# Channel 0's filters shifted by TensorE, read from eight partitions, with products of zeros and other loads at the start

## The chip, the cores and the metric

One core of one Trainium2 chip. The metric is the device time of one execution in microseconds (us), lower is better; for the kernel before, the median of three runs is 884.42 us (883.73 to 887.07).

## The reference, cut to what is computed

Two layers in a row on x of shape (4, 64, 256, 256): 4 images (b), 64 channels (c), 256 by 256 places. All is fp32.

```
# layer 0: a long convolution whose filter is separable, one for each channel
h_X, h_Y = filter(z, X weights), filter(z, Y weights)      # 256 places x 64 channels each
filter: h = sin(freq * (z @ w1 + b1)); h = sin(freq * (h @ w2 + b2)); h = sin(freq * (h @ w3 + b3))
        (h @ wo) * exp(-t * |deltas|)
k[c, i, m] = h_X[i, c] * h_Y[m, c]
y = causal 2D convolution of x[b, c] with k[c], cut to 256 x 256 (the reference does it by FFTs of 512 x 512)
x0 = y + x * bias[c]

# layer 1
scores = x0 @ x0.T / 16                                    # for each image and channel, 256 x 256
red = sum over t of scores[s, t] * weights[c, s, t]        # one number for each row s
y = x0 + red
out = batch norm of y over (b, s, d) for each channel, times gamma[c], plus beta[c]
```

Because the filter is an outer product, the convolution is two products with triangular Toeplitz matrices, one along each axis: z = (Toeplitz of h_Y) on x, then x0 = (Toeplitz of h_X) on z.

## The kernel before

**Preparation (lines 84 to 173).** The small filter network runs once, for all channels, on a transposed z (33 x 256) in two halves of 128 places. For each of three layers and each half, TensorE (PE) multiplies by a 128 x 128 matrix that holds the X and Y weights as blocks (line 131), VectorE (DVE) adds the bias and scales (134), finds the nearest whole number of turns (138) and subtracts it (139), and ScalarE (ACT) takes the sine (141). The biases and the frequencies arrive in fb_sb; line 123 makes a factor of them first. What all 64 channels need then goes this way: a last product (158), times the decay (161), into g_sb; lines 170 write it to g_dram, a DRAM tensor with four copies, each copy's row read later from another start.

**Toeplitz tiles.** A channel's tile `toep` (tag of `hs[c]`) has 128 partitions, two filters (index a: 1 is used by conv_z, 0 by conv_x0) and 256 places: partition p holds the filter put p places on, and partitions 64 to 127 repeat 0 to 63. For channels from 1 on it is read from g_dram by four DMAs of 16 partitions (load_h, line 187), and ACT copies the lower half down (copy_h, line 192). Channel 0 doesn't wait for DRAM: lines 143 to 155 compute its two filters with the weights of that one channel on all 128 columns, so that each partition holds the same filter; two DMAs a filter then read one partition each (0 and 64) at 32 starts, one element apart, into partitions 0 to 31 and 32 to 63 of `hs[0]`. DVE copies these down (line 163). At the end of the preparation three products that nobody reads run on PE (lines 165 to 167, tile `idle`, one buffer).

**Channels.** For each channel, conv_z (line 210) multiplies blocks of xt, the input, by the Toeplitz tile; ACT copies the result from PSUM to the tile z (copy_z, line 219), in two halves m of two blocks each. conv_x0 (line 233) multiplies z by the Toeplitz tile; DVE adds x times the bias (line 240) and makes x0. `gram` (line 270) makes the scores, of which DVE takes the weighted sums (290, 294, 304), GpSimd the sums over partitions, and then means, squares, scaling and output follow for earlier channels. All products use quarters of the PE array: 64 rows and 64 columns, four beside each other.

**Order.** The order is written out by hand; nothing is planned. The loop of channel c issues conv_x0 of c, then conv_z of c + 1, then gram of c, so that PE always has work whose inputs are old. Before the loop stand conv_z of channel 0 and its copies. Loads are all issued on SyncE's queue (SP), in the order of the program: input tiles (load_xt) three channels ahead, Toeplitz rows two ahead, weights (load_w) one ahead. In the preparation ACT's queue carries the weights of the network, one of the two reads per filter of channel 0 and one of the two writes to g_dram. Each DMA takes one of eight semaphores, and an issue waits until the DMA that had it last is done.

**PSUM.** The preparation's pool `fps` uses four buffers for `ph`, three for `ph0` and one for the idle products; it is given back before `ps`, eight buffers of one bank, is opened for the channels. A conv_z or a conv_x0 takes four of them.

Of the kernel before, what the change touches and what calls it, by code (L numbers as in the profile page):

```python
# [16 lines left out]
P = 128  # L17
EMB = 33
# [19 lines left out]
def conv_scores_bn_kernel(  # L38
# [3 lines left out]
    wl: bass.AP,  # L42
    zT: bass.AP,
    fw: bass.AP,
# [38 lines left out]
    ctx.enter_context(tc.manual_schedule())  # L83
    zT_sb = const.tile([EMB, S], F32, name="zT_sb")
    nc.sync.dma_start(zT_sb, zT)
    fw_sb = const.tile([P, 4, P], F32, name="fw_sb")
    nc.scalar.dma_start(fw_sb[:EMB, 0, :], fw[:EMB, 0, :])
    fb_sb = const.tile([P, 4], F32, name="fb_sb")
    nc.sync.dma_start(fb_sb, fb)
    nc.scalar.dma_start(fw_sb[:, 1:, :], fw[:, 1:, :])  # L90
    eps = const.tile([P, 1], F32, name="eps")
    nc.vector.memset(eps, BN_EPS)
    ones = const.tile([P, H], F32, name="ones")
    nc.vector.memset(ones, 1.0)

    warm = const.tile([P, 1], F32, name="warm")
# [24 lines left out]
    hs[0] = ld.tile([P, 2, GW], F32, tag="toep", name="toep_0")  # L121
    with tc.tile_pool(name="fps", bufs=4, space=PSUM) as fps:
        nc.vector.tensor_scalar(turns, fb_sb[:, 3:4], 1.0 / (2.0 * math.pi), None, ALU.mult)

        halves = [zT_sb[:, bass.ts(n, P)] for n in range(2)]
        for layer in range(3):
            for n in range(2):
                rhs = halves[n]
                K = rhs.shape[0]
                ph = fps.tile([P, P], F32, tag="ph", name=f"ph_{layer}_{n}")  # L130
                nc.tensor.matmul(ph, lhsT=fw_sb[:K, layer, :], rhs=rhs, start=True, stop=True)  # L131

                a = wk.tile([P, P], F32, tag="fa", name=f"fa_{layer}_{n}")
                nc.vector.tensor_scalar(  # L134
                    a, ph, fb_sb[:, layer : layer + 1], turns, ALU.add, ALU.mult
                )
                k = wk.tile([P, P], F32, tag="fk", name=f"fk_{layer}_{n}")
                nc.vector.tensor_scalar(k, a, ROUND, None, ALU.add)
                nc.vector.scalar_tensor_tensor(a, k, ROUND, a, ALU.subtract, ALU.subtract)  # L139
                h = wk.tile([P, P], F32, tag="fh", name=f"fh_{layer}_{n}", bufs=4)  # L140
                nc.scalar.activation(h, a, AF.Sin, scale=-PI2)
                halves[n] = h
        for a in (1, 0):
            ph = fps.tile([P, S], F32, tag="ph0", name=f"ph0_{a}", bufs=3)
            for n in range(2):
                weights = fw_sb[:, 3, a * C : a * C + 1].to_broadcast([P, P])
                nc.tensor.matmul(  # L147
                    ph[:, bass.ts(n, P)], lhsT=weights, rhs=halves[n], start=True, stop=True
                )
            nc.vector.tensor_tensor(g0_sb[:, a, :S], ph, decay0_sb[:, a], ALU.mult)  # L150
            for n in range(2):
                row = g0_sb[H * n : H * n + 1, a, 32 * n :]
                src = bass.AP(row.tensor, row.offset, [row.ap[0], [1, 32], [1, S]])
                queue = nc.scalar if n else nc.sync
                queue.dma_start(hs[0][bass.ts(n, 32), a, :S], src)
        ph = fps.tile([P, S], F32, tag="ph0", name="ph_out", bufs=3)
        for n in range(2):
            nc.tensor.matmul(
                ph[:, bass.ts(n, P)], lhsT=fw_sb[:, 3, :], rhs=halves[n], start=True, stop=True
            )  # L160
        nc.vector.tensor_tensor(g_sb[:, :S], ph, decay_sb, ALU.mult)
        for a in (1, 0):
            nc.vector.tensor_copy(hs[0][H:, a, :S], hs[0][:H, a, :S])

        for n in range(3):
            idle = fps.tile([P, 3, P], F32, tag="idle", name=f"idle_{n}", bufs=1)
            nc.tensor.matmul(idle, lhsT=fw_sb[:, 3, :], rhs=fw_sb[:, 1:, :], start=True, stop=True)  # L167
    for a in (1, 0):
# [494 lines left out]
```

## Time and profile before

| What | Value |
|---|---|
| median of three runs | 884.42 us |
| profiled execution, its own time | 883.99 us |
| its span, first to last instruction | 882.2 us |
| mean granted clock of TensorE | 0.992 |
| DMA over the span | 169.68 MB, mean 192 GB/s |
| 0 to 16.8 us: PE busy | 11.23 us |
| 26.1 to 30.5 us: PE busy | 4.40 of 4.40 us |
| 200 to 300 us: PE busy | 99.84 of 100 us |
| 840 to 882 us: PE busy | 27.99 us |

The span is what the profiler saw of one execution, from its first to its last instruction; the time of the same execution is 1.8 us longer, which lies outside the instructions. The rows of stretches add up what PE did in them. A product in fp32 appears as two instructions, since PE passes over the data twice. On a timeline row stand start, length, engine, line, operation, tiles and count; in brackets, how long the engine had been idle and what ended it. SPq and ACTq are the queues on which DMAs are issued: a row's length there is the issue, not the transfer. Two tiles in the preparation are named g_sb and two decay_sb in the trace, since g0_sb and decay0_sb lose their number.

### The profile page before, as it was taken

To read this page: it belongs to the slowest core of one execution; us is meant where nothing else is said; L and a number is where in the kernel's file an instruction comes from. 1 tells how busy PE (TensorE), PEld (TensorE's weight loads), DVE (VectorE), ACT (ScalarE), POOL (GpSimd) and SP (SyncE) were. 2 spreads that over 40 slices of the span, in tenths; PEclk is the share of its full clock that TensorE was granted. 3 is DMA by queue.
4 is the path that set the end of the run, shared out by engine and by line. 5 is a ranking of instruction groups with operands and counts; after the bars stand their busy time and mean duration, and the time that the engine had idled before them with its cause. 6 is when DMAs were issued, how large, how long until landed. Compare 5 with 4: busy or idle time off the path is not lost.

```text
span 882.2 us, 55900 instructions
## 1 busy us (share of the span) xinstructions
PE 860.4 (98%) x24678; PEld 827.0 (94%) x24678; DVE 754.9 (86%) x2642; ACT 616.7 (70%) x1212; POOL 425.1 (48%) x195
## 2 busy tenths in 40 slices
PE   7999999999999999999999999999999999999993
PEld 5999999999999999999999999999999999999992
DVE  3588988998898898898898898898898898898885
ACT  2257767767777777776776776776776776776784
POOL 0236446546545545645645644645645545645600
PEclk9999999999999999999999999999999999999996
DMA  6525556556556556556556565556556556556534
GB/s 187 178 88 176 198 197 211 198 190 212 198 196 212 192 199 208 197 194 211 192 199 209 197 197 202 196 193 207 191 192 210 183 201 206 201 193 206 182 124 169
DMA packets 89913, 169.68 MB, mean 192 GB/s; under 512 B 10566, under 2 KB 11784, under 8 KB 89672
## 3 DMA queue, kind: packets, MB, share of 16 engines
q1 hardware_dynamic: 89116, 165.51, 55.5%
q8 instruction: 194, 3.18, 1.5%
q10 hardware_dynamic: 556, 0.61, 0.2%
q14 instruction: 47, 0.39, 0.1%
HBM read 98.18 MB, written 67.76 MB: 188 GB/s over the span
## 4 chain that ended last, share of the span: by engine, by line
PE 97%; DVE 1%; ACT 0%; issue 0%; DMA 0%; ACTq 0%; SPq 0%; DVEq 0%
PE p L210 32%; PE p L233 32%; PE g L270 32%; PE rp L341 0%; PE rp L346 0%; PE idle L167 0%; DVE x L355 0%; DMA fb_sb<-in_fb 0%; ACT o L406 0%; PE ph L147 0%; PE ph L131 0%; DVE fa L134 0%; DVE fa L139 0%; DVE junk L290 0%; ACT z L219 0%
## 5 line engine op out<-in xcount | busy, mean ns | idle before, releaser
L312 POOL PARTITION_ALL_REDUCE rd<-sp x61 | 373.5, 6122 | 183.8 <-DVE sp L304 183.8
L233 PE MATMUL p<-toep,z 64*64 64x256 f32 (+3 forms) x8192 | 300.6, 296 | 1.2 <-issue 1.0
L210 PE MATMUL p<-toep,xt 64*64 64x256 f32 (+3 forms) x8192 | 299.8, 296 | 0.4 <-issue 0.2
L233 PEld LDWEIGHTS p<-toep,z 64*64 64x64 f32 x8192 | 285.5, 133 | 14.4 <-issue 2.8
L270 PE MATMUL g<-x 64*64 64x192 f32 (+1 forms) x8192 | 298.1, 296 | 0.4 <-issue 0.3
L210 PEld LDWEIGHTS p<-toep,xt 64*64 64x64 f32 x8192 | 282.9, 133 | 12.2 <-PE idle L167 0.7
L270 PEld LDWEIGHTS g<-x 64*64 64x64 f32 x8192 | 283.3, 133 | 2.8 <-issue 1.0
L290 DVE SCALAR_TENSOR_TENSOR junk<-g,w 128x192 f32<-128x192 f32 x512 | 161.1, 352 | 86.5 <-PE g L270 86.5
L406 ACT ACTIVATE o<-x,sh,g 128x512 f32<-128x512 f32 x253 | 203.5, 808 | 0.0
L240 DVE SCALAR_TENSOR_TENSOR x<-xt,chan_sb,p 128x512 f32<-128x512 f32 x256 | 174.1, 742 | 9.0 <-PE p L233 9.0
L219 ACT COPY z<-p 128x512 f32<-128x512 f32 x256 | 134.7, 577 | 31.1 <-PE p L210 31.1
L366 ACT ACTIVATE sq<-x,mom 128x1024 f32<-128x1024 f32 x128 | 146.3, 1143 | 5.4 <-DVE x L355 2.0
L326 DVE SCALAR_TENSOR_TENSOR x<-x,rd 128x1024 f32<-128x1024 f32 x122 | 144.2, 1220 | 0.1
L304 DVE SCALAR_TENSOR_TENSOR sp<-eye_sb,red,pr 128x128 f32<-128x128 f32 x488 | 138.1, 346 | 0.0
L330 POOL PARTITION_ALL_REDUCE mom<-mom x61 | 24.3, 399 | 235.0 <-DVE x L326 230.9
L294 DVE SCALAR_TENSOR_TENSOR pr<-g,w 128x256 f32<-128x256 f32 x256 | 107.5, 420 | 0.0
L319 ACT COPY rd<-rd 64x512 f32<-64x512 f32 x61 | 37.6, 616 | 91.1 <-POOL rd L312 91.1
L361 ACT ACTIVATE mom<-mom 128x1 f32<-128x1 f32 x62 | 18.3, 295 | 77.3 <-POOL mom L330 77.3
L192 ACT COPY toep<-toep 64x512 f32<-64x512 f32 x63 | 38.9, 617 | 39.9 <-DMA toep<-g_dram 26.4
L290 DVE DVE_READ_ACCUMULATOR junk<-g,w 128x1 f32 x512 | 42.6, 83 | 0.0
L372 POOL PARTITION_ALL_REDUCE tot<-mom x62 | 29.7, 480 | 9.5 <-ACT sq L366 9.5
L366 ACT ACTIVATION_READ_ACCUMULATOR sq<-x,mom 128x1 f32 x128 | 23.8, 186 | 0.0
(60 smaller groups left out, 212.0 us busy)
## 6 DMA issues: line engine op xcount, KB each, us to landing
xt<-in_xT SPq DMA_DIRECT2D x256, 256.0 KB
out<-o SPq DMA_DIRECT2D x256, 256.0 KB
w<-in_wl SPq DMA_DIRECT2D x64, 320.0 KB
toep<-g_dram SPq DMA_DIRECT2D x252, 36.0 KB
g_dram<-g_sb SPq DMA_DIRECT2D x1, 320.0 KB
g_dram<-g_sb ACTq DMA_DIRECT2D x1, 320.0 KB
decay_sb<-in_decay SPq DMA_DIRECT2D x1, 256.0 KB
fw_sb<-in_fw ACTq DMA_DIRECT2D x1, 192.0 KB
```

The source lines that it names most:

```text
L210: nc.tensor.matmul(p1[u][bass.ts(v, H), k, : S - H * i], lhsT=xts[c, v][rows, i, bass.ts(2 * m + k, H)], rhs=toep[rows, 1, H * i : S], sta ...
L219: nc.scalar.copy(zs[c][:, u, bass.ts(m, 2), :], p1[u][:, :, ::-1])
L233: nc.tensor.matmul(p2[v][bass.ts(u, H), i, : S - H * k], lhsT=z[rows, u, k, bass.ts(2 * m + i, H)], rhs=toep[rows, 0, H * k : S], start=(k ...
L240: nc.vector.scalar_tensor_tensor(x0[:, v, part], xt[v][:, part], chan_sb[:, 0, c : c + 1], p2[v][:, :, ::-1], ALU.mult, ALU.add,)
L270: nc.tensor.matmul(gs[u][bass.ts(h, H), o, :], lhsT=xb[rows, v, i, m, :], rhs=xb[rows, v, i, t, :], start=(i == 0), stop=(i == 3),)
L290: nc.vector.scalar_tensor_tensor(junk, g[:, part, :], 1.0 / math.sqrt(S), w[:, 3 * n : 3 * n + 3, :], ALU.mult, ALU.mult, accum_out=red0[: ...
L294: nc.vector.scalar_tensor_tensor(pr[:, b].rearrange("p (t s) -> p t s", s=H), g[:, COL, :], 1.0 / math.sqrt(S), w[:, 6:10, :], ALU.mult, A ...
L304: nc.vector.scalar_tensor_tensor(sp[:, b, part], eye_sb, red0[:, b, n : n + 1], pr[:, b, part], ALU.mult, ALU.add,)
L312: nc.gpsimd.partition_all_reduce(rd.rearrange("p b s -> p (b s)"), sp.rearrange("p b s -> p (b s)"), P, RED.add)
L326: nc.vector.scalar_tensor_tensor(x0[:, v], x0[:, v], 1.0, rd[:, 2 * v, None, :].to_broadcast([P, 4, S]), ALU.mult, ALU.add, accum_out=mom[ ...
L366: nc.scalar.activation(sq, st8[c][0][:, v], AF.Square, bias=mom[:, 5:6], accum_out=mom[:, 6 + v : 7 + v])
L406: nc.scalar.activation(o, y, AF.Identity, bias=sh, scale=g)
```

## The change

- The transposed z and the first layer's weights are one input `zw` and one load on SP; fb_sb is loaded first on ACT's queue, then the other weights `fw`, now of three layers.
- A function `idle` makes products of `ones` (64 columns) by `zeros` that nobody reads: three of 256 columns ahead of the network, one of 64 columns after each of its six products, and seven of 256 columns at the end in place of three with `fw`.
- Channel 0's filters: the 128 output partitions of `ph0` are four groups of 32, and the products of group k are put 16 k places on, so that partition 32 k holds the filter 16 k places on; the rest of `ph0` is set to zero ahead of the network, and `decay0` is put on the same way. Each filter's two DMAs then read four partitions each (0, 32, 64, 96 and 1, 33, 65, 97) at 16 starts and write 64 partitions each, so both halves of `hs[0]` are written and DVE's copies go.
- Channel 0's `w` and channel 1's input are loaded after the writes to g_dram instead of ahead of the network.
- conv_x0 of channel 0 is `first_x0`: all four PSUM banks are taken at once, the products with the first half of z (k of 0 and 1) come first for all rows, then those with the second half, and DVE's additions come after each m of the second half.

The diff, with declarations and the host's arrays cut:

```diff
     ctx.enter_context(tc.manual_schedule())
-    zT_sb = const.tile([EMB, S], F32, name="zT_sb")
-    nc.sync.dma_start(zT_sb, zT)
-    fw_sb = const.tile([P, 4, P], F32, name="fw_sb")
-    nc.scalar.dma_start(fw_sb[:EMB, 0, :], fw[:EMB, 0, :])
+    zw_sb = const.tile([P, P + S], F32, name="zw_sb")
+    nc.sync.dma_start(zw_sb[:EMB], zw[:EMB])
     fb_sb = const.tile([P, 4], F32, name="fb_sb")
-    nc.sync.dma_start(fb_sb, fb)
-    nc.scalar.dma_start(fw_sb[:, 1:, :], fw[:, 1:, :])
+    nc.scalar.dma_start(fb_sb, fb)
+    fw_sb = const.tile([P, 3, P], F32, name="fw_sb")
+    nc.scalar.dma_start(fw_sb, fw)
     eps = const.tile([P, 1], F32, name="eps")
     nc.vector.memset(eps, BN_EPS)
     ones = const.tile([P, H], F32, name="ones")
     nc.vector.memset(ones, 1.0)
+    zeros = const.tile([P, S], F32, name="zeros")
+    nc.vector.memset(zeros, 0.0)
 
     warm = const.tile([P, 1], F32, name="warm")
     nc.scalar.activation(warm, eps, AF.Sin)
...
     nc.sync.dma_start(eye_sb, eye)
     chan_sb = const.tile([P, 3, C], F32, name="chan_sb")
     nc.sync.dma_start(chan_sb.rearrange("p a c -> p (a c)"), chan.to_broadcast([P, 3 * C]))
-    load_w(0)
-    for part in PARTS:
-        load_xt(1, *part)
     g_sb = const.tile([P, GW], F32, name="g_sb")
     nc.vector.memset(g_sb[:, S:], 0.0)
 
...
 
     hs[0] = ld.tile([P, 2, GW], F32, tag="toep", name="toep_0")
     with tc.tile_pool(name="fps", bufs=4, space=PSUM) as fps:
+        def idle(cols, number=1):
+
+            for _ in range(number):
+                none = fps.tile([H, S], F32, tag="none", name="none", bufs=1)
+                nc.tensor.matmul(
+                    none[:, :cols], lhsT=ones, rhs=zeros[:, :cols], start=True, stop=True
+                )
+
+        idle(S, 3)
+
+        SHIFT = 16
+        ph0s = [fps.tile([P, S], F32, tag="ph0", name=f"ph0_{a}", bufs=3) for a in range(2)]
+        for a in (1, 0):
+            nc.vector.memset(ph0s[a][:, S - 3 * SHIFT :], 0.0)
         nc.vector.tensor_scalar(turns, fb_sb[:, 3:4], 1.0 / (2.0 * math.pi), None, ALU.mult)
 
-        halves = [zT_sb[:, bass.ts(n, P)] for n in range(2)]
+        halves = [zw_sb[:EMB, bass.ts(1 + n, P)] for n in range(2)]
         for layer in range(3):
             for n in range(2):
                 rhs = halves[n]
-                K = rhs.shape[0]
+                weights = fw_sb[:, layer - 1, :] if layer else zw_sb[:EMB, :P]
                 ph = fps.tile([P, P], F32, tag="ph", name=f"ph_{layer}_{n}")
-                nc.tensor.matmul(ph, lhsT=fw_sb[:K, layer, :], rhs=rhs, start=True, stop=True)
+                nc.tensor.matmul(ph, lhsT=weights, rhs=rhs, start=True, stop=True)
+                idle(H)
 
                 a = wk.tile([P, P], F32, tag="fa", name=f"fa_{layer}_{n}")
                 nc.vector.tensor_scalar(
...
                 nc.scalar.activation(h, a, AF.Sin, scale=-PI2)
                 halves[n] = h
         for a in (1, 0):
-            ph = fps.tile([P, S], F32, tag="ph0", name=f"ph0_{a}", bufs=3)
+            ph = ph0s[a]
+            weights = fw_sb[:, 2, a * C : a * C + 1].to_broadcast([P, 32])
             for n in range(2):
-                weights = fw_sb[:, 3, a * C : a * C + 1].to_broadcast([P, P])
-                nc.tensor.matmul(
-                    ph[:, bass.ts(n, P)], lhsT=weights, rhs=halves[n], start=True, stop=True
-                )
+                for k in range(4):
+                    first = max(0, P * n - SHIFT * k)
+                    nc.tensor.matmul(
+                        ph[bass.ts(k, 32), first : P * (n + 1) - SHIFT * k], lhsT=weights,
+                        rhs=halves[n][:, first + SHIFT * k - P * n :], start=True, stop=True,
+                    )
             nc.vector.tensor_tensor(g0_sb[:, a, :S], ph, decay0_sb[:, a], ALU.mult)
+
             for n in range(2):
-                row = g0_sb[H * n : H * n + 1, a, 32 * n :]
-                src = bass.AP(row.tensor, row.offset, [row.ap[0], [1, 32], [1, S]])
+                rows = g0_sb[n : n + 97 : 32, a, :]
+                src = bass.AP(rows.tensor, rows.offset, [rows.ap[0], [1, SHIFT], [1, S]])
                 queue = nc.scalar if n else nc.sync
-                queue.dma_start(hs[0][bass.ts(n, 32), a, :S], src)
+                queue.dma_start(hs[0][bass.ts(n, H), a, :S], src)
         ph = fps.tile([P, S], F32, tag="ph0", name="ph_out", bufs=3)
         for n in range(2):
             nc.tensor.matmul(
-                ph[:, bass.ts(n, P)], lhsT=fw_sb[:, 3, :], rhs=halves[n], start=True, stop=True
+                ph[:, bass.ts(n, P)], lhsT=fw_sb[:, 2, :], rhs=halves[n], start=True, stop=True
             )
         nc.vector.tensor_tensor(g_sb[:, :S], ph, decay_sb, ALU.mult)
-        for a in (1, 0):
-            nc.vector.tensor_copy(hs[0][H:, a, :S], hs[0][:H, a, :S])
-
-        for n in range(3):
-            idle = fps.tile([P, 3, P], F32, tag="idle", name=f"idle_{n}", bufs=1)
-            nc.tensor.matmul(idle, lhsT=fw_sb[:, 3, :], rhs=fw_sb[:, 1:, :], start=True, stop=True)
+        idle(S, 7)
     for a in (1, 0):
         queue = nc.scalar if a else nc.sync
         queue.dma_start(
             g_dram[:, :, a, :].rearrange("n c g -> c n g"),
             g_sb[bass.ts(a, C), None, :].to_broadcast([C, COPIES, GW]),
         )
+    load_w(0)
+    for part in PARTS:
+        load_xt(1, *part)
     gam = const.tile([P, C], F32, name="gam")
     nc.vector.tensor_scalar(gam, chan_sb[:, 1, :], -0.5, None, ALU.mult)
 
...
     def conv_x0(c, z, parts=range(2)):
 
 
-        xt = [xts[c, v] for v in range(2)]
-        toep, x0 = hs[c], st8[c][0]
+        toep = hs[c]
+        if not c:
+            first_x0(z)
+            return
         for m in parts:
             p2 = [ps.tile([P, 2, S], F32, tag="ps", name=f"p2_{c}_{m}_{v}") for v in range(2)]
             for i in range(2):
...
                             lhsT=z[rows, u, k, bass.ts(2 * m + i, H)],
                             rhs=toep[rows, 0, H * k : S], start=(k == 0), stop=(k == 3),
                         )
-            for v in range(2):
-                part = bass.ts(m, 2)
-                nc.vector.scalar_tensor_tensor(
-                    x0[:, v, part], xt[v][:, part], chan_sb[:, 0, c : c + 1],
-                    p2[v][:, :, ::-1], ALU.mult, ALU.add,
-                )
+            add_bias(c, m, p2)
+
+    def add_bias(c, m, p2):
+        for v in range(2):
+            part = bass.ts(m, 2)
+            nc.vector.scalar_tensor_tensor(
+                st8[c][0][:, v, part], xts[c, v][:, part], chan_sb[:, 0, c : c + 1],
+                p2[v][:, :, ::-1], ALU.mult, ALU.add,
+            )
+
+    def first_x0(z):
+
+        toep = hs[0]
+        p2 = [
+            [ps.tile([P, 2, S], F32, tag="ps", name=f"p2_0_{m}_{v}") for v in range(2)]
+            for m in range(2)
+        ]
+        for half in range(2):
+            for m in range(2):
+                for i in range(2):
+                    for k in range(2 * half, 2 * half + 2):
+                        for t in range(4):
+                            v, u = t % 2, t // 2
+                            rows = bass.ts(v, H)
+                            nc.tensor.matmul(
+                                p2[m][v][bass.ts(u, H), i, : S - H * k],
+                                lhsT=z[rows, u, k, bass.ts(2 * m + i, H)],
+                                rhs=toep[rows, 0, H * k : S],
+                                start=(i == 0 and k == 0), stop=(i == 1 and k == 3),
+                            )
+                if half:
+                    add_bias(0, m, p2[m])
...
+    zw = np.zeros((P, P + S), np.float32)
+    zw[:EMB, P:] = a["L0_conv_z"][0, ::-1].T
+    decay0 = np.zeros((4, 32, 2, S), np.float32)
+    for k in range(4):
+        decay0[k, :, :, : S - 16 * k] = decay[::C, ::-1][:, 16 * k :]
+    decay0 = decay0.reshape(P, 2, S)
+    fw = np.zeros((P, 3, P), np.float32)
```

More of the change, by code (lines that the diff above doesn't have):

```diff
@@ L42, in conv_scores_bn_kernel @@
     wl: bass.AP,
-    zT: bass.AP,
+    zw: bass.AP,
     fw: bass.AP,
@@ L608 @@
     decay = np.concatenate([dec, dec / np.float32(FFT)], 0)
-    fw = np.zeros((P, 4, P), np.float32)
+    zw = np.zeros((P, P + S), np.float32)
[5 more added lines that the diff above has]
+    fw = np.zeros((P, 3, P), np.float32)
     fb = np.zeros((P, 4), np.float32)
@@ L613 @@
         lo, hi = i * C, (i + 1) * C
-        fw[:EMB, 0, lo:hi] = a[f"L0_conv_{n}w1"]
-        fw[lo:hi, 1, lo:hi] = a[f"L0_conv_{n}w2"]
-        fw[lo:hi, 2, lo:hi] = a[f"L0_conv_{n}w3"]
-        fw[lo:hi, 3, lo:hi] = a[f"L0_conv_{n}wo"]
+        zw[:EMB, lo:hi] = a[f"L0_conv_{n}w1"]
+        fw[lo:hi, 0, lo:hi] = a[f"L0_conv_{n}w2"]
+        fw[lo:hi, 1, lo:hi] = a[f"L0_conv_{n}w3"]
+        fw[lo:hi, 2, lo:hi] = a[f"L0_conv_{n}wo"]
         for j, b in enumerate(("b1", "b2", "b3")):
@@ L639 @@
         "wl": wl,
-        "zT": a["L0_conv_z"][0, ::-1].T,
+        "zw": zw,
         "fw": fw,
@@ L643 @@
         "decay": decay[:, ::-1],
-        "decay0": np.broadcast_to(decay[::C, ::-1], (P, 2, S)),
+        "decay0": decay0,
         "chan": np.concatenate(
```

## The prediction

> **What bounds the kernel now.** I read the page's first and fourth parts, then the chain in order of time over the first 45 us, the timeline of that stretch, the rows of single lines, and the DMA view of two short windows.
>
> ```profile
> PE 860.4 (98%) x24678; PEld 827.0 (94%) x24678; DVE 754.9 (86%) x2642; ACT 616.7 (70%) x1212; POOL 425.1 (48%) x195
> PE 97%; DVE 1%; ACT 0%; issue 0%; DMA 0%; ACTq 0%; SPq 0%; DVEq 0%
> ```
>
> TensorE is 98% busy and is 97% of the chain. What the change touches ends where channel 0's products do, so it can shift only the start of a stream that runs without holes afterwards.
>
> ```profile
> 16.70 0.04 issue
> 16.74 4.67 PE p L210 x128
> 21.41 1.06 ACT z L219 x2
> 22.47 0.04 issue
> 22.51 3.71 PE p L233 x84
> ...
> 26.34 4.36 PE p L210 x107
> 30.70 4.35 PE g L270 x121
> 35.05 4.36 PE p L233 x113
> ```
>
> Columns: start, length, what. The stream begins at 16.74; channel 1's first product (conv_z) starts in earnest at 26.34, 9.60 us later. Undisturbed, the two products take 4.36 each, and I allow 8.8 with the filling of the pipe; 0.8 is the hole at 21.41, where PE waits for z's second half. From 26.34 on blocks follow each other, so the effect of the change is the shift of this 26.34.
>
> ```profile
> 3.50 0.15 DVE L123 TENSOR_SCALAR turns<-fb_sb 128x1 f32<-128x1 f32 x1 [2.34 <-DMA fb_sb<-in_fb]
> 3.77 0.41 DVE L134 TENSOR_SCALAR fa<-ph,fb_sb,turns 128x128 f32<-128x128 f32 x1
> ...
> 11.88 1.37 SPq L155 DMA_DIRECT2D toep<-g_sb  x2
> ...
> 12.89 3.79 PE L167 MATMUL idle<-fw_sb 128*128 128x384 f32 x6
> ...
> 15.46 0.29 DVE L163 COPY toep<-toep 64x256 f32<-64x256 f32 x1 [1.90 <-DMA toep<-g_sb]
> ...
> 19.02 2.67 SPq L187 DMA_DIRECT2D toep<-g_dram  x4
> ...
> 24.87 0.62 ACT L192 COPY toep<-toep 64x512 f32<-64x512 f32 x1 [2.41 <-DMA toep<-g_dram]
> ```
>
> Before 16.74 there is one chain. The filters start at 3.77 (call it F). Channel 0's filter rows go out at 11.88 (call it T), arrive at 15.46 = T+3.6, and are copied down by 15.75. PE starts only at 16.74 = T+4.9, because three idle products run until 16.70. A second chain leaves T too: the filters of all channels go to DRAM, SP reads channel 1's back from 19.02 = T+7.1, and ACT's copy makes them ready at 25.49 = T+13.6, only 0.85 us before PE wants them. An earlier start of PE alone is therefore worth little more than that 0.85.
>
> ```profile
> L131 PE MATMUL ph<-fh,fw_sb x8: 421/501/582, 5.2 to 8.7; 128*128 128x128 f32 x8
> L167 PE MATMUL idle<-fw_sb x6: 486/718/955, 12.9 to 16.2; 128*128 128x384 f32 x6
> ```
>
> Min, median and max ns. One shape runs 955 early and 486 late: PE is at half speed until about 15.2, where the trace's first clock record (full) stands. Before that record the page's clock row means nothing.
>
> ```profile
> DMA packets 20, 0.04 MB, mean 46 GB/s; under 512 B 4, under 2 KB 4, under 8 KB 20
> ```
>
> The DMA view of 20.4 to 21.2: the first load of channel 1's filter rows, 16 data packets and four completions, so four DMA engines carried it.
>
> **What the skill says.** "TensorE: Matmul & The Clock Gate", Part 1: the array runs at half clock until a free-running window of about 3.4 us has been busy. The trace agrees: half speed from 2.59 through gappy work, full at 15.2 after a nearly gapless stretch from 11.8. How busy is enough it doesn't show; counting streaming and weight loads, 67% (8.4 to 11.8) was not, 92% (11.8 to 15.2) was. "DMA: Bandwidth & Descriptors", on why a DMA increments its semaphore by 16: the number of engines is the largest up to 16 that divides the outermost sizes of both sides. The four completions above (an outermost 4) agree. "SBUF — State Buffer", Door 1: partitions 0-3 and 32-35 share one DMA port, 64-67 and 96-99 another, some 27 GB/s each. The packets of the old reads agree: 64 of 1 KB from partition 0 took about 2.6 us, 64 from partition 64 about 2.3, that is 36 to 40 ns each per port.
>
> **The change part by part.**
>
> *Three zero products first.* A product of 64 weight columns by 256 costs, at half clock, two passes of 0.427 (a pass of 128 columns is 0.213 apart in L131's rows), about 0.1 of weight load, 0.207 until the result and 0.06 for the wait on its predecessor (the one buffer "none", as L167's one buffer does now: weights idle 1.2 there): 1.2 us. They start when the memset of zeros is done, about 1.25 (the memset of 128 columns takes 0.17, this one twice as many), and end near 4.9. Queued behind them on PE is layer 0's first product, whose data are there at about 2.45. It then takes 0.79 as now (2.59 to 3.38): F becomes about 5.45, 1.7 later. The earlier biases (fb first on ACT's queue, perhaps 0.6 sooner) and the merged z and weights hide behind this and are worth nothing.
>
> *Clock.* If these products count as busy, the clock comes between 4.7 and 8.1 (a whole window after 1.25). A layer now lasts 2.23 (6.00 to 8.22). At full clock its product falls from 0.80 to 0.49, and DVE's two halves (0.95 each) bound the layer at 1.95: two layers give 0.56, of which I take 0.5. The idle products of 64 columns after each product (0.3 to 0.4) fall into PE's gaps: the halves come 0.91 apart and a product at half clock takes 0.8 with its latency.
>
> *Shifted filters by PE.* Instead of two products of 128 columns per filter, eight narrow ones, four beside each other in column groups; L346's pairs at the end (8 instructions in 0.61) show that such pairs overlap. From the last sine to the multiplication it is 0.88 now (10.55 to 11.43), at full clock about 0.55: 0.3 gained. New T: 11.88 + 1.7 - 0.5 - 0.3 = 12.8.
>
> *The reads.* Each filter now moves 2 x 64 KB instead of 2 x 32. The eight source partitions (0, 1, 32, 33, 64, 65, 96, 97) lie on the same two ports as before, and the outermost 4 of the source lets four engines work. By ports: 64 packets of 38 ns, 2.4 us; by engines: 32 packets of 46 ns, the duration of an undisturbed one, 1.5. I take 2.4. First packet at T+1.2 (issue 0.63, then 0.56 as z's load shows), so filter 1 is there at T+4.0 with 0.4 until the consumer sees it (15.07 to 15.46 now), filter 0 at T+6.4, in time for its use at T+9. The two copies of 0.29 go, as does the queueing behind channel 1's inputs (the first packet left at 13.18, T+1.3; 0.1 at most).
>
> *Seven zero products.* They follow the last filter product at about T+0.35. At full clock one takes 0.68 (a pair of L341 alone takes 0.62, plus the wait), so the stream starts at T+5.1 even though its data are there at T+4.0.
>
> *x0 by halves.* Half 0 needs only z's first half, copied long before: the 0.8 hole goes. The additions of x0's first rows come later, but gram needs them only 4.4 us on. By this path channel 1's conv_z can start at 12.8 + 5.1 + 8.8 = 26.7.
>
> *Channel 1's filters.* On the four engines the reads last until T+6.1 (both filters, 4.9 us). Then come the writes to DRAM: 32 packets each of 55 to 75 ns, 1.8 to 2.4, done at T+8.2; SP wakes at T+8.5. The moved loads (w of channel 0, channel 1's xt, 1.34 MB) now lie in SP's ring behind those writes: 84 KB per engine, 42 packets of 0.08, until T+11.6. The four filter loads queue behind them on the same four engines: 16 packets of 93 ns, T+13.1, seen at T+13.5; ACT's copy ends at T+14.2 (T+13.6 now). That is 12.8 + 14.2 = 27.0, later than 26.7: this wait ends last. Issuing the moved loads costs SP five times 0.45, inside its wait for DRAM.
>
> *Sum.* 27.0 against 26.34 is +0.6 or 0.7; I take +0.6. The profiled execution took 883.99 (span 882.2), so 884.6; the median shown is 0.43 above it: 885.0.
>
> **Rivals.**
> 1. The zero products hold nothing back (no wait on each other, or an early clock). F is then about 3.3 to 3.8 and T about 11. Channel 1's filters still bind at T+14.2 = 25.2: -1.1; if they come as soon after T as now (13.6), -1.8: about 883. For it: the biases do come early. Against it: L167's waits and PE's fixed order. Even this can't reach 4 us.
> 2. The ports or the DRAM writes are worse, and channel 1's filters are ready 1.5 to 2.5 later than I put them: +2 to +3, 887. For it: four engines carry everything in turn. Against it: their packets are short ones.
> 3. Slower: zero products keep PE too little busy (streaming and weight loads 78% by the figures above, between 67 and 92), and the clock is never granted before the stream. T is then 13.6; seven products of 1.2 from T+0.8 end at 22.9, and the stream's first window at half clock costs 2.5 more: 22.9 + 8.8 + 2.5 = 34.2, +8, 892. It decides once more than four of the seven run at half clock.
>
> **How the numbers follow.** Forecast 0.58, rival 1 0.20, rival 2 0.12, rival 3 0.10. A change of 0.5% is 4.4 us, about what a measurement of this kernel tells from none. The forecast and rivals 1 and 2 lie within it, rival 3 is above; 0.09 is left for a gain that I can't see in these 26 us, taken from the first three: faster 0.09, same 0.81, slower 0.10. The range runs from rival 1 (882.6) to rival 2 (888.0).
>
> **What would show it.** F near 5.4 and the clock record between 4.7 and 8.1 (right), or F near 3.5; seven zero products 0.68 apart ending at T+5.1; filter reads in four engines' packets 38 ns apart per port; no wait for z in channel 0's second product; ACT's copy of channel 1's filter ending after channel 0's products. A start of channel 1 before 24 would make the prediction wrong, and so would any change from channel 2 on.

## The result and the profile after

| | before | after |
|---|---|---|
| median of 22 runs each | 885.54 us | 890.67 us |
| ratio after / before, 95% interval | | 1.0057 (1.0041 to 1.0073) |
| profiled execution, own time | 883.99 us | 889.87 us |
| its span | 882.2 us | 888.0 us |
| start of gram of channel 0 in the chain | 30.70 | 35.67 |

The change made the kernel 5.1 us slower, where 885.0 (between 882.6 and 888.0) had been forecast. The last row of the table is the yardstick for everything below: gram of channel 0 starts 4.97 us later, and from there to the end of the span the two take 851.5 (882.2 - 30.70) and 852.3 us, nearly the same. So the 5 us were lost ahead of that point. By its interval the loss is 3.6 to 6.5 us; its parts are read from one profiled execution of each kernel.

The page of the kernel after, first part (busy time by engine) and fourth part (share of the chain that ended last):

```profile
PE 869.3 (98%) x24728; PEld 842.8 (95%) x24728; DVE 754.9 (85%) x2643; ACT 617.7 (70%) x1212; POOL 425.1 (48%) x195
...
PE 97%; DVE 2%; issue 0%; ACT 0%; ACTq 0%; DVEq 0%
```

The same 98% and 97% as before: shares of a whole span can't show a loss in its first 36 us, and products of zeros count as busy. The chain in order of time does show it (start, length, what; kernel after):

```profile
1.28 1.13 PE none L125 x2
2.45 1.13 PE none L125 x2
3.63 1.11 PE none L125 x2
4.74 0.72 PE ph L143 x2
...
12.61 1.49 PE ph L162 x21
14.10 1.15 PE ph_out L175 x4
15.26 1.06 PE none L125 x2
...
16.36 1.12 PE none L125 x2
...
17.52 0.66 PE none L125 x2
...
21.04 4.59 PE p L225 x128
25.64 4.44 PE p L279 x128
30.07 0.47 issue
30.55 4.90 PE p L225 x84
...
35.67 4.13 PE g L313 x112
```

`none` are the products of zeros: 1.13 each ahead of the network and still at the first two of the seven, 0.66 only from 17.52. The stream, channel 0's conv_z and all that follows it on PE, starts at 21.04 (16.74 before). Channel 0's two products then take 9.03 without the hole for z, PE waits 0.47, and channel 1's conv_z starts slowly. Why it waits stands not in the chain but in the timeline (start, length, engine, line, operation, tiles, count; kernel after):

```profile
5.50 0.41 DVE L147 TENSOR_SCALAR fa<-ph,fb_sb,turns 128x128 f32<-128x128 f32 x1 [2.67 <-PE ph L143]
...
13.79 1.40 SPq L172 DMA_DIRECT2D toep<-g_sb  x2
...
15.74 1.56 SPq L182 DMA_DIRECT2D g_dram<-g_sb  x1
...
17.36 2.03 SPq L78 DMA_DIRECT2D w<-in_wl  x1
...
19.44 4.99 SPq L72 DMA_DIRECT2D xt<-in_xT  x4
...
24.54 2.67 SPq L202 DMA_DIRECT2D toep<-g_dram  x4
...
30.42 0.62 ACT L207 COPY toep<-toep 64x512 f32<-64x512 f32 x1 [3.65 <-DMA toep<-g_dram]
```

So F = 5.50, T = 13.79, and channel 1's filters are ready (ACT's copy ended) at 31.04 = T+17.25; before it was T+13.6. Two chains leave T, and **both** are late:

| | before | forecast | after |
|---|---|---|---|
| F, first bias addition | 3.77 | 5.45 | 5.50 |
| T, filter reads go out | 11.88 | 12.8 | 13.79 |
| stream starts | T+4.9 | T+5.1 | T+7.25 |
| SP issues channel 1's filter loads | T+7.1 | T+8.5 | T+10.8 |
| channel 1's filters ready | T+13.6 | T+14.2 | T+17.25 |

The single DMA packets in the trace show the second chain. Each filter read has packets of 1 KB; the two filters together have 128 before and 256 after.

| kernel | read packets | first start to last end, us | mean ns of one | writes to g_dram, first start to last end |
|---|---|---|---|---|
| before | 128 | 13.17 to 16.09 | 210 | 15.32 to 18.68 |
| after | 256 | 15.08 to 20.66 | 70 | 17.96 to 24.09 |
| eight ports, below | 256 | 15.13 to 18.87 | 53 | 17.08 to 21.45 |

Before, the two reads of a filter (outermost size 32) spread over 16 engines. The 210 ns are a mean of two kinds: SP's packets, from partition 0, took 356 ns each, ACT's, from partition 64, 64 ns. After, four engines work with 70 ns each; the first three reads follow one another, the fourth overlaps the third. The reads end 2.7 us later relative to T (T+6.9, not T+4.2). The writes begin among them, at T+4.2, and end at T+10.3, not T+6.8. Each write is in sixteen parts: of the one that lands last, twelve had landed by 21.60 in the kernel after and the other four came between 23.17 and 24.42. Four is the number of engines that carried the reads.

### The profile page after: what moved, and what is told of

It is laid out like the page before. It is cut to its first block, busy times and chain, and to the rows that moved or that the text cites. A ratio compares the mean times of both kernels' runs of the same rounds, so it can differ in the third digit from the quotient of the medians.

```text
span 888.0 us, 56001 instructions
## 1 busy us (share of the span) xinstructions
PE 869.3 (98%) x24728; PEld 842.8 (95%) x24728; DVE 754.9 (85%) x2643; ACT 617.7 (70%) x1212; POOL 425.1 (48%) x195
## 4 chain that ended last, share of the span: by engine, by line
PE 97%; DVE 2%; issue 0%; ACT 0%; ACTq 0%; DVEq 0%
PE p L225 32%; PE g L313 31%; PE p L250 31%; PE none L125 1%; PE p L279 0%; PE ph L143 0%; PE rp L384 0%; DVE junk L333 0%; PE rp L389 0%; DVE x L398 0%; DVE x L369 0%; ACT o L449 0%; DVE pr L337 0%; PE ph L162 0%; PE ph_out L175 0%
## 5 line engine op out<-in xcount | busy, mean ns | idle before, releaser
L225 PE MATMUL p<-toep,xt 64*64 64x128 f32 (+3 forms) x8192 | 303.3, 297 | 0.7 <-PE p L279 0.5
L250 PE MATMUL p<-toep,z 64*64 64x128 f32 (+3 forms) x8064 | 297.9, 297 | 1.6 <-issue 1.6
L225 PEld LDWEIGHTS p<-toep,xt 64*64 64x64 f32 x8192 | 290.2, 133 | 7.8 <-issue 1.4
L250 PEld LDWEIGHTS p<-toep,z 64*64 64x64 f32 x8064 | 289.1, 133 | 8.1 <-issue 3.0
L313 PEld LDWEIGHTS g<-x 64*64 64x64 f32 x8192 | 286.8, 133 | 1.3 <-issue 0.5
L260 DVE SCALAR_TENSOR_TENSOR x<-xt,chan_sb,p 128x512 f32<-128x512 f32 x256 | 174.1, 743 | 14.7 <-PE p L279 13.6
```

Source lines behind the costliest of these rows:

```text
L225: nc.tensor.matmul(p1[u][bass.ts(v, H), k, : S - H * i], lhsT=xts[c, v][rows, i, bass.ts(2 * m + k, H)], rhs=toep[rows, 1, H * i : S], sta ...
L250: nc.tensor.matmul(p2[v][bass.ts(u, H), i, : S - H * k], lhsT=z[rows, u, k, bass.ts(2 * m + i, H)], rhs=toep[rows, 0, H * k : S], start=(k ...
L260: nc.vector.scalar_tensor_tensor(st8[c][0][:, v, part], xts[c, v][:, part], chan_sb[:, 0, c : c + 1], p2[v][:, :, ::-1], ALU.mult, ALU.add,)
L313: nc.tensor.matmul(gs[u][bass.ts(h, H), o, :], lhsT=xb[rows, v, i, m, :], rhs=xb[rows, v, i, t, :], start=(i == 0), stop=(i == 3),)
```

## The experiments

Three series, each on one chip and beside the kernel before on that chip: medians of before 886.77 (first four), 895.38 (next four), 885.54 (last four). "Scores" is the start of gram of channel 0 in the chain.

A clock record is the trace's note that the granted clock changed; "record at" names the first one, which stands for full clock.

**1. Without the zero products of the head**

```diff
-        idle(S, 3)
...
-                idle(H)
```

> The changed kernel without the three zero products ahead of the network and without the one after each of its products; the seven at the end stay. Landmark: the start of channel 0's scores in the chain, 30.70 us before and 35.67 after. Theory (zero products ahead of the network delay it, and everything behind hangs on the network): the first bias addition starts at about 3.3 instead of 5.50, the filter reads go out at 11.4 instead of 13.79, and the whole rest moves up by the same 2.3: scores at about 33.3, time 2.3 us below the changed kernel. Rival A (PE's end is what counts: the clock now comes later, so the seven products at the end run cold and the stream starts no earlier than 20): scores at 35 or later, time unchanged. Rival B (the zero products did help the clock): layers longer than the 2.26 of the changed kernel; I expect none.

Ratio 1.0024 (1.0006 to 1.0042). The chain of this kernel:

```profile
18.15 4.59 PE p L222 x128
22.75 4.44 PE p L276 x128
27.18 1.12 issue
28.30 4.90 PE p L222 x83
...
33.43 3.57 PE g L310 x90
```

F is 3.40 and T 11.57, 2.2 earlier, and so are the scores (33.43). The stream starts 2.9 earlier, yet PE waits 1.12 at 27.18: ACT's copy of channel 1's filters ends at 28.80. The head's zero products cost 2.2 us of T and don't bring the clock: its first record stands at 13.52 here, without them, and at 17.32 in the kernel after.

**2. The moved loads back ahead of the network**

```diff
+    load_w(0)
+    for part in PARTS:
+        load_xt(1, *part)
     g_sb = const.tile([P, GW], F32, name="g_sb")
...
-    load_w(0)
-    for part in PARTS:
-        load_xt(1, *part)
     gam = const.tile([P, C], F32, name="gam")
```

> The changed kernel with channel 0's w and channel 1's input loaded ahead of the network again. Theory (SP's slow issue of these loads, 17.36 to 24.43, and their packets hold the loads of channel 1's filters): these are issued at 23.4 or earlier instead of 24.54, ACT's copy ends by 29.9 instead of 31.04, the stream loses its wait, scores at about 34.4 instead of 35.67, time 1 to 1.3 us lower. Rival (the filter reads on four engines alone hold the writes to DRAM): issue at 24.4 as in the changed kernel, scores at 35.5, time unchanged.

Ratio 1.0037 (1.0014 to 1.0059). Scores at 34.40 (-1.27). The timeline:

```profile
23.82 2.62 SPq L202 DMA_DIRECT2D toep<-g_dram  x4
...
29.14 0.62 ACT L207 COPY toep<-toep 64x512 f32<-64x512 f32 x1 [3.06 <-DMA toep<-g_dram]
```

With nothing to issue in between, SP still waits until 23.82, because the last write lands only at 23.77 (24.42 in the kernel after). The issue starts 0.72 earlier than there, and the filters are then ready another 0.56 sooner.

**3. No wait between the zero products**

```diff
+        none = fps.tile([H, S], F32, tag="none", name="none", bufs=1)
+
         def idle(cols, number=1):
-
             for _ in range(number):
-                none = fps.tile([H, S], F32, tag="none", name="none", bufs=1)
```

> The changed kernel with one PSUM tile for all zero products, so that none waits for its predecessor. Theory (waits make them long): three take 2.6 instead of 3.5, first addition at 4.7 instead of 5.50, reads at 13.0 instead of 13.79; the seven end at 18 to 19 instead of 21.0, but the stream then waits for channel 1's filters, which come 0.8 earlier at most: scores at 34.9, time 0.8 lower. Rival A (the start of the stream is the bound): scores at 33. Rival B (without waits PE is busy enough for the clock during the network): a clock record before 9, layers of 1.95, reads at 12.3, scores at 34 or less.

Ratio 1.0040 (1.0024 to 1.0057). The seven take 4.41 and the stream starts at 19.00, 2.04 earlier, but the scores come at 36.91, later than in the kernel after. The chain:

```profile
28.45 1.75 issue
30.21 6.43 PE p L225 x87
...
36.91 0.16 PE g L313
```

and the view by stretches (columns: stretch, length, busy time and count of PE, PEld, DVE, ACT and POOL, granted clock, DMA share, GB/s):

```profile
28.30:30.20 1.90, 0.04 (x1) 0.02 (x1) 1.90 (x4) 0.12 (x1) 0.00 (x0) 1.00 0.82 269
30.60:34.00 3.40, 3.40 (x46) 3.01 (x48) 0.00 (x0) 0.10 (x1) 0.00 (x0) 0.50 0.92 268
34.00:60.00 26.00, 26.00 (x771) 25.57 (x768) 16.16 (x64) 8.08 (x16) 6.55 (x2) 1.00 0.30 99
```

PE idles 1.9 us for channel 1's filters and then runs 3.4 us at clock 0.50. An earlier stream gave nothing, so channel 1's filters end last (ready at 30.70 here); and waiting for them can cost the clock as well. The expectation missed this second price.

**4. The kernel before, with first_x0 alone**

```diff
+        if not c:
+            first_x0(z)
+            return
...
```

> The kernel before with channel 0's x0 by halves of z alone. Theory: the stream starts at 16.74 as before, channel 0's two products take 9.0 instead of 9.6, channel 1's filters are ready at 25.5, so its conv_z starts at 25.8 instead of 26.3: scores at 30.15 instead of 30.70, time 0.5 lower (0.06%). Rival (the hole only moves, to the additions or to channel 1's filters): scores at 30.6 or later, time the same.

Ratio 0.9990 (0.9973 to 1.0006). From the start of the stream to the scores it takes 13.33 instead of 13.96, without a hole:

```profile
15.80 4.59 PE p L210 x128
20.39 4.37 PE p L264 x128
24.76 4.37 PE p L210 x128
29.13 4.52 PE g L298 x127
```

The gain of 0.63 is in the trace; the time can't resolve it. That the stream also began 0.94 earlier here is no part of the edit: the preparation's first addition came 0.27 sooner (3.50), and the clock's record stands at 13.36 instead of 15.21.

**5 and 6. When do zero products bring the clock?** Nine in the head in place of three, once on one tile (as in 3) and once each on a tile of its own, which waits.

```diff
-        idle(S, 3)
+        idle(S, 9)
```

> The changed kernel with nine zero products of 256 columns ahead of the network instead of three, all on one PSUM tile, so none waits: a measurement of the clock. They keep PE streaming without a hole from 1.3 to about 9 at half clock (0.85 each). Theory (products of zeros count as work, and what was missing was a whole window without holes): the clock record stands between 4.7 and 8.1, products after it take half the time, and the network's layers last about 1.95. Rival (zeros, or 64 columns of the array, do not count): no record before 13, all nine at 0.85. The time is worse than the changed kernel's in either case.

> The changed kernel with nine zero products ahead of the network instead of three, each waiting for its predecessor as in the changed kernel: 1.17 each at half clock, streaming 73% of it, from 1.3 to at most 11.8. Theory (with the waits PE streams too little for the clock): no clock record before 11.8. Rival (the waits don't matter, three were only too few to fill a window): a record between 4.7 and 8.1, and products of 0.70 after it.

One execution each, 901.1 and 902.04, which tells nothing of the time. All instructions of the zero products' line from 0 to 12 us (min, median, max ns; span of starts), first on one tile, then with waits:

```profile
L125 PE MATMUL none<-zeros,ones x28: 222/379/686, 1.3 to 11.1; 128*64 128x256 f32 x18, 128*64 128x64 f32 x10
```

```profile
L125 PE MATMUL none<-zeros,ones x18: 634/662/689, 1.3 to 11.1; 128*64 128x256 f32 x18
...
  PEld none L125: 7.1, 8
```

Without waits the clock record stands at 4.26, and durations fall from 634 to 379 ns: zeros do count. With waits, each of eight lets the weights load wait 0.9 (the last line: 7.1 in all), 10.5 us pass at half clock, and the record comes at 24.53. The first kernel then lost the clock again (stretches, columns as above):

```profile
4.30:11.00 6.70, 5.77 (x30) 3.61 (x28) 3.42 (x12) 0.93 (x3) 0.00 (x0) 1.00 0.57 180
11.10:17.90 6.80, 6.23 (x46) 4.04 (x47) 3.25 (x11) 0.93 (x3) 0.00 (x0) 0.50 0.05 12
```

At full clock the network's short products with one of 64 columns each leave PE too empty to keep it: with pass times half of those at half clock, an estimate, PE streams data for only about a third of the window from 7.67 to 11.09.

**7. Eight ports instead of two** for channel 0's filter reads:

```diff
-                rows = g0_sb[n : n + 97 : 32, a, :]
+                rows = g0_sb[16 * n : 16 * n + 109 : 36, a, :]
```

> The changed kernel with the filter reads from partitions 0, 36, 72, 108 and 16, 52, 88, 124 instead of 0, 32, 64, 96 and 1, 33, 65, 97: the same bytes by the same four engines, but from eight ports instead of two by the skill's table. Theory (two ports bind the reads): the 1 KB packets take about 46 ns instead of 70, the four reads end about 2.6 us sooner after their issue, SP issues the moved loads sooner, channel 1's filters are ready at 28.5 instead of 31.04, the stream no longer waits for them: scores at 34.4 instead of 35.67, time 1.3 lower. Rival (the four engines bind): packets of 70 ns as now, scores at 35.6, time unchanged.

Every partition of a group holds the same filter, so partitions 0, 36, 72, 108 and 16, 52, 88, 124 serve as well. Ratio 1.0028 (1.0007 to 1.0049), that is 2.2 us above before instead of 5.1. SP's packets take 46 ns instead of 70, SP's read of filter 1 takes 0.73 us instead of 1.48, and the timeline shows the gain handed on:

```profile
21.88 2.60 SPq L202 DMA_DIRECT2D toep<-g_dram  x4
...
27.83 0.62 ACT L207 COPY toep<-toep 64x512 f32<-64x512 f32 x1 [1.64 <-DMA toep<-g_dram]
```

Filters ready 2.6 us earlier (28.45), and now the stream is last: its two products end at 29.45 and conv_z of channel 1 follows without a wait. The scores start at 34.30, 1.37 before the kernel after; a hole of 1.12 at 34.90 that the profile charges only to "issue" eats most of it in this one profile. Whether it returns in other executions isn't known.

**8. The parts that help, without those that cost**: the edits of 1, 2 and 7, and three zero products at the end for seven; first_x0 and the shift by PE stay.

```diff
-        idle(S, 3)
...
-                idle(H)
...
+                rows = g0_sb[16 * n : 16 * n + 109 : 36, a, :]
...
-        idle(S, 7)
+        idle(S, 3)
```

> The changed kernel without the zero products ahead of and in the network, with the moved loads back ahead of it, with the reads from partitions on eight ports, and with three instead of seven zero products at the end: what the findings so far point to. Theory: reads go out at 11.5, channel 1's filters are ready at about 25 instead of 31.04 (25.49 in the kernel before), the stream starts at 16.4: scores at 29.5 to 30 against 30.70 before, time about 1 us (0.1%) below the kernel before. Rival A (four engines still hold the writes to DRAM): filters at 27 or later, scores at 31.5, about 1 us above the kernel before. Rival B (with three zero products the stream starts at half clock): scores 1 to 2 us later than by the theory.

Ratio 0.9962 (0.9936 to 0.9988): faster than both kernels. Its chain:

```profile
11.81 3.70 DMA toep<-g_sb
...
16.32 4.59 PE p L222 x128
20.91 4.37 PE p L276 x128
25.28 4.40 PE p L222 x105
...
29.74 4.34 PE g L310 x120
```

The filters of channel 1 are ready at 25.10 = T+13.3, just ahead of 25.28, and no hole is left. The scores come 0.96 earlier than before; the median says 3.4, with an interval from 1.1 to 5.7, so about 1 is what the trace supports. The stream ran at full clock from its start because the record stands at 15.71; experiment 9 shows that this isn't sure.

**9. The last kernel with two ports again**

```diff
-                rows = g0_sb[16 * n : 16 * n + 109 : 36, a, :]
+                rows = g0_sb[n : n + 97 : 32, a, :]
```

> The combined kernel b1 with the filter reads from two ports again (partitions 0, 32, 64, 96 and 1, 33, 65, 97). Theory (ports bind the reads, and these hold the writes to DRAM): packets of 70 ns instead of 46 to 54, the reads end 2 us later, channel 1's filters are ready about 2.3 us later than in b1 (25.1), at 27.4, and the scores begin at 31.8 to 32 instead of 29.74. Rival (in b1 only the missing zero products and the loads matter): filters ready at 25 to 25.5, scores at 30.

Ratio 1.0002 (0.9981 to 1.0022). Filters ready at 27.95 = T+16.1, that is 2.8 later after T, with read packets of 69 ns. Scores at 32.59. Part of that is a stream that began at half clock (record at 20.49): the same three zero products as in 8 stand ahead of it, at much the same times, and this time brought no clock.

**10. The kernel before with late loads**: only the loads moved, as the change moves them.

```diff
-    load_w(0)
-    for part in PARTS:
-        load_xt(1, *part)
     g_sb = const.tile([P, GW], F32, name="g_sb")
...
+    load_w(0)
+    for part in PARTS:
+        load_xt(1, *part)
     gam = const.tile([P, C], F32, name="gam")
```

> The kernel before with channel 0's w and channel 1's input loaded after the writes to DRAM, nothing else. Theory (the late loads hurt by standing before channel 1's filter loads on SP and in the rings): SP issues the filter loads 0 to 1 us later than 19.02, their packets queue behind 1.3 MB, ACT's copy ends 1 to 2 us later than 25.49, the stream waits for it, scores at 31.5 to 32.5 instead of 30.70, time about 1 us above the kernel before. Rival (the loads only get in the way of the filter reads, so late is better): reads land sooner, scores at 30.5.

Ratio 0.9995 (0.9970 to 1.0021). The filters are ready at 26.60 = T+14.8 (T+13.6 before), the scores at 31.23, 0.53 late. The time can't show so little; the timeline does: four issues of xt, 0.43 each elsewhere, take 4.14 (up to 1.70 for one). They are over at 19.04, and the filter loads follow at 19.36, when the last write has landed (19.34). So of the 1.1 by which the filters are late, 0.34 lies ahead of the loads' issue and the rest behind it, where the moved packets are.

```profile
14.90 4.14 SPq L72 DMA_DIRECT2D xt<-in_xT  x4
...
19.36 2.68 SPq L187 DMA_DIRECT2D toep<-g_dram  x4
```

**11 and 12. How many zero products?** The kernel of 8 with none at all, and with one tile, one product ahead of the network, one of 128 columns after each of its products.

```diff
-        idle(S, 3)
```

```diff
+        none = fps.tile([H, S], F32, tag="none", name="none", bufs=1)
...
+        idle(S)
...
+                idle(P)
```

> The combined kernel b1 without any zero product. Theory (only channel 1's filters bind; what PE does before is of no account): the stream starts as soon as filter 1 has landed, about 15.5, at half clock, and full clock comes within 3.4 to 6.8 us of it; it reaches channel 1's product by 25 to 26 and the scores at 29.7 to 30.5, time within 0.1% of b1's gain over the kernel before. Rival (the zero products are needed for the clock): stream at half clock for a whole window or two, scores at 31 or later, time 1 to 2 us worse than b1.

> The combined kernel b1 with zero products that don't wait for each other (one PSUM tile): one of 256 columns before the network, which ends about when z arrives, one of 128 after each of the network's products, three at the end. PE then streams about 74% of the network's time; 69% was too little (nine with waits), and the window that brought the clock in the changed kernel held about 80%. Theory A (74% is enough): a clock record before 9, layers under 2.1, reads at 11.3, scores 0.5 us before b1's 29.74. Theory B (too little): the clock comes as in b1, after 12, layers of 2.25 to 2.35, reads at 12, scores at 30.2.

Ratios 1.0006 (0.9986 to 1.0027) and 0.9988 (0.9972 to 1.0004). Without any, the stream starts cold and its first product takes 7.15:

```profile
15.35 7.15 PE p L221 x128
22.50 4.37 PE p L275 x128
```

Scores at 31.37, 1.6 later than in 8, where three zero products in the wait for the filters brought the clock; in 9 the same three did not, and the scores came at 32.59. So the 1.6 can be had, but not for certain. Filling the network made a layer longer (2.69 instead of 2.23) and brought no earlier clock (record at 16.78). It is no test of the 74% that the expectation names (its 69 and 80% are 73 and 75% as counted below): with four passes of 0.213 in 1.345 us PE streamed 63% of the time. Scores at 30.72, a miss against the 30.2 hoped for.

## Why the prediction was wrong

**Right:** F (5.45 forecast, 5.50 measured); that the zero products wait on each other (1.17 apart); that the stream's data come long before the stream starts (filter 1 seen at T+4.0 by the forecast, at T+4.5 in fact, the stream at T+7.25); the hole for z, which goes (9.03 for both products, and experiment 4 by itself); that channel 1's filters end last; that a late start of this one chain is the whole effect.

**Wrong, the step "Clock": "If these products count as busy, the clock comes between 4.7 and 8.1".** They count, but with their waits the array streams data for only 73% of the time (two passes of 0.427 in 1.17), and that is not enough: in experiment 6 the clock didn't come in 10.5 us of them, and without waits it came within 3 us. In the network it is 57% (two passes of 0.213 and two of 0.107 in 1.13). In the 3.41 us ahead of the record at 17.32 it is 75% (four passes of 0.213 at L175 and four of 0.427 at L125). The forecast counted weight loads as busy too and took the middle between its two known points, 67 and 92%, for enough. By its own count the network stood at 78% and got no clock, and the window ahead of the record at 83%. With the clock went the 0.5 of two layers and the 0.3 of the narrow products: from F to T it took 8.29, about as before (8.11), instead of 7.35, and T is 13.79 instead of 12.8. It also put two of the seven at half clock and moved their start from T+0.35 to T+1.4, which made the stream T+7.25 instead of T+5.1. Rival 3 named this cause, but needed more than four of the seven at half clock; it was two.

"TensorE: Matmul & The Clock Gate" (Part 1) of the Trainium skill speaks of a free-running busy window of about 3.4 us without saying how busy. Counting such windows back from the first record in all fourteen traces (a pass streams until 0.21 before its end), none with up to 73% of streaming brought the clock and none with 75% or more failed to. With weight loads counted as well the two groups part just as cleanly, at 81 and 83%, so these runs give a border but not what is counted. And as the windows don't start with the kernel, it is partly luck what falls into one: the three zero products of experiment 9 filled the window from 13.67 to 17.08 to 72%, those of experiment 8, which began only 0.07 sooner, shared theirs (12.30 to 15.71) with the last filter product, and it came to 81%.

**Wrong, the step "Channel 1's filters": "On the four engines the reads last until T+6.1 ... done at T+8.2".** The reads lasted until T+6.9 and the writes until T+10.3. The reads were priced too low: each of the two ports passed 128 packets in 5.6 us, 44 ns each, where the forecast took 38. It had read the old reads from partition 0 as 2.6 us; they ran from 13.17 to 16.00, and 64 packets in that time are 44 ns each as well. The writes were put on engines that are free after the reads, for 2.1 us; they ran in among the reads and for 3.4 us after them. 0.65 of that goes with the moved loads (experiment 2); for the rest it is most likely the engines of the reads that held them, since twelve of sixteen parts of the last write were through almost 3 us before the end. The trace doesn't name engines. Experiment 7 says what the 70 ns of a packet are: 46 with eight ports. "SBUF — State Buffer", Door 1, has that partitions such as 0 and 32 share a port, and the measurement agrees: four readers on two ports have half the rate of four readers on four (1.48 us a read, not 0.73). This was rival 2's cause, sized there at 1.5 to 2.5 and in fact 3.0. Rival 1, in which the zero products hold nothing back, fell: F was 5.50, and without them T came 2.2 earlier (experiment 1).

**Wrong in size, without effect: "Issuing the moved loads costs SP five times 0.45, inside its wait for DRAM".** It took 7.07 us (17.36 to 24.43), up to 2.03 for a single DMA, but it lay inside the wait: the last write landed at 24.42 and the filter loads were issued at 24.54. In experiments 1, 3, 7 and 10 SP had been done 0.2 to 0.5 before that issue. So the moved loads cost by their packets and not by their issue: without them the last write lands 0.65 sooner, the filter loads go out 0.72 sooner, and these take another 0.56 less (experiment 2). Why the issue is slow stays open. A backlog on four engines isn't needed for it: in experiment 10 the reads spread over sixteen.

**The sum.** Filters ready were forecast at 27.0 and came at 31.04: 1.0 by T, 3.0 by the chain behind it (2.2 ahead of the loads' issue, and 0.8 behind it: 6.5 to ready, where 5.7 was forecast). The remaining 0.3 is a slow start of conv_z (5.12 from its start to the scores instead of 4.36, from 30.55), whose products of the lower half wait for ACT's copy. The two errors aren't additive. With T+17.25 behind the forecast T the scores would be near 34.7; with the stream at 21.04 and the filters as forecast, near 34.4 (21.04 + 9.03 + 4.36). Against the 30.70 of before each error alone costs nearly 4 us, and so undoing one (experiments 2, 3, 7) gives 1.4 us at most; only experiment 1, which moves T itself, moves both chains.

The chain behind T adds up from its parts: 17.25, less 2.6 for the ports (experiment 7; 2.8 between 8 and 9), less 1.3 for the moved loads (1.28 in experiment 2, 1.2 in 10), is 13.3, what experiment 8 has and 0.3 less than before.

## What to carry to other kernels

Longer reads that spare a copy don't help when the source partitions share a port and the packets crowd on few DMA engines: count packets for each engine and each port, then ask what is queued behind them, for that is where the cost appears. Products that only keep TensorE's clock up belong in a wait that exists anyway and never in front of real work (2.2 us here). Let them follow each other without a wait: nine that did brought the clock within 3 us, nine that waited not in 10.5. Where two chains leave one point, cost both to their ends, since repairing one shows little while the other is as late.

## What the hardware showed that was not expected

- A DMA issue that takes 0.43 us on SP took up to 2.09 us (experiment 1) right behind the filter reads and the writes to DRAM (five in 7.07 us after, four in 4.14 us in experiment 10), and now and then later (1.47 at 22.92 in experiment 8). It held up no load of channel 1's filters by more than 0.1, and its cause isn't known.
- One wait of 1.9 us on TensorE, in an otherwise full stream, was followed by 3.4 us at half clock (experiment 3); the Trainium skill ("TensorE: Matmul & The Clock Gate", "Why this matters for your kernels") puts the limit at gaps of some 3 us. A wait of 1.12 in experiment 1 was not followed by half clock, though it left at most 67% of its window (27.17 to 30.59, counted on from the record) for work: keeping the clock asks for less than getting it.
- The first reads on ACT's and on SP's queue, issued at the same time, didn't take turns packet by packet: ACT's ran from 15.08 to 16.58, and only then did SP's begin, at 16.39 on the first engine that was through (kernel after). The last two reads did overlap.
